# Cross-attention and an int8-style feed-forward: key products by seven block products for eight, sums and scaling on GpSimd, one pool of PSUM banks, a new order of steps

## The chip, the cores and the metric

The kernel runs on one core of a Trainium2 chip. The metric is the device time of one execution in microseconds (us), the median of several runs. The core has a matmul engine (TensorE, "PE" in the profile, its weight loads "PEld"), a vector engine (VectorE, "DVE"), an activation engine (ScalarE, "ACT"), a general engine (GpSimd, "POOL") and a queue that issues all DMAs here (SyncE, "SP"). Matmul results land in PSUM, which has eight banks of 512 fp32 columns per partition; everything else lies in SBUF or in DRAM.

## The reference, cut to what matters

Eight batches of 112 tokens of 512 features attend to a context of 375 rows of 256 features, and then go through a feed-forward layer with operands rounded as if to int8. There are 16 heads of 128.

```python
def attention(x, ctx):                  # x is layer-normed, per batch
    q = (x @ Wq).reshape(Sq, 16, 128)
    k = (ctx @ Wk).reshape(375, 16, 128)
    v = (ctx @ Wv).reshape(375, 16, 128)
    q, k = rmsnorm(q, gq), rmsnorm(k, gk)          # over each head's 128
    p = softmax(q k^T / sqrt(128))                 # per head
    return (p v).reshape(Sq, 2048) @ Wo
x = x + attention(layernorm(x), ctx)
x = x + ffn(layernorm(x))               # rows of x and all of W1, W2 scaled and rounded to +-127,
                                        # gelu between, hidden width 2048
```

## The kernel before

The batches go in four pairs p. The heads go in four groups of 4 heads (512 columns of Wq, Wk, Wv). A pair and a group of heads make one of 16 groups G; a group and one of its two batches make one of 32 units u. All of it is fp32 up to the feed-forward layer; each fp32 matmul of the program shows as two in the profile.

For one unit: `keys` multiplies three tiles of 128 context rows (the context is padded from 375 to 384) with the group's 512 columns of Wk, each tile in two products that accumulate over the 256 features (L650). `key_keep` copies the tile out of PSUM (ScalarE, L670), `key_squares` squares it (ScalarE, L675), `key_sums` adds the squares per head (VectorE, L681), the root steps (names `ka`, `kb`, `ke`, `kd`: Ln and Exp on ScalarE, small VectorE operations) make 1/rms, `key_norm` scales the tile (VectorE, L688), `key_blocks` transposes its blocks of 32 (VectorE, L698), `key_send` writes them to DRAM in four DMAs and `key_fetch` reads them back as the transposed keys kT. For the very first unit the transposition is done on TensorE. `queries` makes q in the same manner (L532); the 112 tokens of the last batch lie in the 16 spare rows of the other seven batches' tiles of 128, so it needs no query products of its own. `scores` multiplies q and kT (L758, one bank per head), `score_max` finds maxima in PSUM (VectorE, L771), `score_exp` takes the exponential (ScalarE, L780), `scale_probs` divides by the sum (ScalarE, L791), `prob_blocks`, `prob_send` and `prob_fetch` transpose the probabilities by way of DRAM (pz, pd, pT). `weigh` multiplies the probabilities with the context itself (L860), `weigh_keep` copies the result (L871); per group, `values` multiplies it with Wv (L887), `value_keep` copies, `project` multiplies with Wo (L910) and `project_add` sums the groups in aT (VectorE, L926). When a pair's four groups are done, the result is transposed back, added to x, normalized, rounded and sent through the feed-forward layer (`hidden` L1080, `gelu` L1096, `output` L1159). The last unit and the last two batches use TensorE transposes in place of those through DRAM.

Tiles are taken from pools with a fixed number of buffers; a new tile of a tag waits until the oldest one's readers are done. The context tiles cT and c have 3 buffers each, the key tiles 2 of three tiles. PSUM is divided into two pools of 4 banks: `ps_sc` for score tiles and `ps_mm` for all else. GpSimd does four memsets at the start and two maxima over partitions.

The order is written out by hand. `step` gives each piece of work a short name (k0..k2 `keys`, kc `key_keep`, kq `key_squares`, kr `key_sums`, kn `key_norm`, kt `key_blocks`, ks and kf the DMAs, s `scores`, x `score_max`, e `score_exp`, n `scale_probs`, w `weigh`, o `values`, p `project`, h `hidden`, g and ge `gelu`, f.. the feed-forward statistics). `play` runs through a script of such words, `name.number`, once for each pair, and `in_written_order` then ties every instruction of TensorE, VectorE, ScalarE and SP to the one before it on its engine. So each engine works strictly in the script's order, and an instruction that waits holds all behind it on its engine.

## Time and profile before

| | us |
|---|---|
| median of 3 runs | 721.83 |
| lowest, highest | 721.05, 722.44 |
| span of the profiled execution | 718.5 |
| TensorE busy | 702.7 |
| VectorE busy | 537.3 |
| ScalarE busy | 433.6 |
| GpSimd busy | 2.4 |
| key products (L650) | 171.8 |
| weighing (L860) | 152.3 |
| projection (L910) | 101.8 |
| queries (L532) | 100.2 |
| scores (L758) | 92.4 |

The span runs from the first to the last instruction of the one execution that was profiled; the profile has no time of that execution around the span. Busy time is a union of intervals, and the ends of matmuls are modelled, so a matmul that stands alone looks longer than one in a row. "Idle before" is time that an engine waited ahead of a group of instructions, with what ended the wait.

### The profile page before, as it was taken

The page shows a single profiled execution, that of the slowest core. Times are in us where ns is not written, and L with a number is a line of the kernel's source. Part 1 is how long each engine was busy: PE and PEld are TensorE (multiplying, and loading weights), DVE is VectorE, ACT ScalarE, POOL GpSimd, SP SyncE. Part 2 cuts the span into 40 slices and gives each one's busy share as a digit, 9 for nine tenths or more (in the row PEclk, how much of TensorE's full clock was granted, in tenths as well). Part 3 has the DMA queues.
Part 4 walks back from the last instruction along what each step waited for, and adds up shares of the span by engine and source line. Part 5 has one row for each costly group of instructions (what it writes and reads, how often), then busy time and mean ns, then how long its engine had stood idle before and what let it go on. Part 6 is the DMA issues. An engine that isn't in the chain of part 4 may idle for free.

```text
span 718.5 us, 8555 instructions
## 1 busy us (share of the span) xinstructions
PE 702.7 (98%) x2398; PEld 413.3 (58%) x2410; DVE 537.3 (75%) x1234; ACT 433.6 (60%) x1129; POOL 2.4 (0%) x10
## 2 busy tenths in 40 slices
PE   9999999999999999999999999999999999999976
PEld 4444456655657564745656465564657455667742
DVE  6997888887876677747857787868774898964395
ACT  5677576636475756556466556666755566627325
POOL 0000000000000000000000000000000000000000
PEclk9999999999999999999999999999999999999999
DMA  8799999989988999999898989999999889998201
GB/s 304 266 280 298 294 298 282 301 268 290 282 308 244 293 285 313 269 275 310 227 289 286 295 265 287 287 240 305 292 257 291 237 256 272 259 290 282 34 1 44
DMA packets 131246, 187.85 MB, mean 261 GB/s; under 512 B 34864, under 2 KB 90800, under 8 KB 130560
## 3 DMA queue, kind: packets, MB, share of 16 engines
q1 hardware_dynamic: 131200, 187.32, 85.1%
q8 instruction: 19, 0.31, 0.2%
q14 instruction: 27, 0.22, 0.1%
HBM read 124.55 MB, written 59.45 MB: 256 GB/s over the span
## 4 chain that ended last, share of the span: by engine, by line
PE 85%; DVE 5%; ACT 4%; DMA 3%; SPq 1%; issue 1%; POOL 0%; ACTq 0%; DVEq 0%; POOLq 0%
PE pkk L650 19%; PE pu L860 17%; PE pw L910 13%; PE pq L532 12%; PE sc L758 10%; PE po L887 6%; PE py L1159 2%; PE ph L1080 2%; DMA pT<-pd 1%; PE pkk L660 1%; DMA kT<-kd 1%; ACT probs L780 1%; DMA qr<-q 1%; DMA qss<-s 1%; ACT qsq L547 1%
## 5 line engine op out<-in xcount | busy, mean ns | idle before, releaser
L650 PE MATMUL pkk<-wk,cT 128*128 128x512 f32 x372 | 171.8, 593 | 0.3 <-DVE hid L1089 0.3
L860 PE MATMUL pu<-pT,c 128*128 128x448 f32 (+1 forms) x384 | 152.3, 540 | 1.0 <-DMA pT<-pd 1.0
L860 PEld LDWEIGHTS pu<-pT,c 128*128 128x128 f32 (+1 forms) x384 | 72.5, 190 | 71.3 <-issue 61.7
L780 ACT ACTIVATE probs<-sc,bias,rq 112x375 f32<-112x375 f32 x128 | 84.1, 663 | 47.8 <-DVE bias L773 47.8
L650 PEld LDWEIGHTS pkk<-wk,cT 128*128 128x128 f32 x372 | 70.0, 190 | 72.3 <-issue 60.9
L910 PEld LDWEIGHTS pw<-oT,wo 128*128 128x128 f32 x544 | 98.2, 190 | 9.8 <-issue 6.5
L910 PE MATMUL pw<-oT,wo 128*128 128x224 f32 (+1 forms) x544 | 101.8, 343 | 0.6 <-ACT oT L897 0.6
L532 PE MATMUL pq<-wq,xnT 128*128 128x512 f32 x224 | 100.2, 592 | 0.0
L758 PE MATMUL sc<-kT,qT 128*112 128x384 f32 x256 | 92.4, 486 | 0.3 <-DMA kT<-kd 0.2
L670 ACT COPY kk<-pkk 128x512 f32<-128x512 f32 x96 | 55.2, 580 | 58.6 <-DVE kz L698 25.6
L797 DVE STREAM_TRANSPOSE pz<-probs 128x384 f32<-128x384 f32 x120 | 63.7, 558 | 21.1 <-ACT probs L791 18.2
L791 ACT ACTIVATE probs<-probs,inv 112x375 f32<-112x375 f32 x128 | 72.1, 605 | 8.9 <-DVE inv L788 8.9
L771 DVE TENSOR_REDUCE top<-sc 112x1 f32<-112x375 f32 x128 | 63.8, 535 | 18.0 <-PE sc L758 17.5
L681 DVE TENSOR_REDUCE kss<-ksq 128x4 f32<-128x512 f32 x96 | 63.1, 668 | 14.0 <-ACT ksq L675 14.0
L532 PEld LDWEIGHTS pq<-wq,xnT 128*128 128x128 f32 x224 | 42.4, 190 | 49.6 <-issue 46.5
L758 PEld LDWEIGHTS sc<-kT,qT 128*112 128x112 f32 x256 | 44.7, 177 | 38.9 <-issue 16.7
L675 ACT ACTIVATE ksq<-kk 128x512 f32<-128x512 f32 x96 | 59.5, 628 | 6.4 <-DVE kss L681 6.0
L688 DVE TENSOR_TENSOR kk<-kk,rk 128x512 f32<-128x512 f32 x96 | 62.9, 675 | 0.5
L698 DVE STREAM_TRANSPOSE kz<-kk 128x512 f32<-128x512 f32 x93 | 62.3, 690 | 0.9 <-issue 0.4
L871 ACT COPY wc<-pu 128x448 f32<-128x448 f32 x64 | 33.5, 531 | 36.6 <-PE pu L860 36.6
L887 PEld LDWEIGHTS po<-wc,wv 128*128 128x128 f32 x272 | 49.1, 190 | 8.0 <-issue 4.1
L887 PE MATMUL po<-wc,wv 128*128 128x224 f32 (+1 forms) x272 | 53.1, 344 | 0.0
(122 smaller groups left out, 590.8 us busy)
## 6 DMA issues: line engine op xcount, KB each, us to landing
kd<-kz SPq DMA_DIRECT2D x124, 192.0 KB, 4.0
kT<-kd SPq DMA_DIRECT2D x31, 768.0 KB, 6.4
pT<-pd SPq DMA_DIRECT2D x30, 672.0 KB, 6.1
pd<-pz SPq DMA_DIRECT2D x90, 192.0 KB, 4.4
wq<-in_wq SPq DMA_DIRECT2D x16, 1024.0 KB, 7.7
wo<-in_wo SPq DMA_DIRECT2D x16, 1024.0 KB, 7.8
wv<-in_wv SPq DMA_DIRECT2D x16, 512.0 KB, 5.8
wk<-in_wk SPq DMA_DIRECT2D x15, 512.0 KB, 6.2
```

Of the source, the lines that this page charges most:

```text
L532: nc.tensor.matmul(pq[:, :GW], T["xnT", p][:, k, i * P : (i + 1) * P], T["wq", G][:, k, :], start=(k == 0), stop=(k == KC - 1),)
L650: nc.tensor.matmul(pk[:, :GW], T["cT", batch_of(u)][:, k, j * P : (j + 1) * P], T["wk", u // BP][:, k, :], start=(k == 0), stop=(k == KCC ...
L681: nc.vector.tensor_reduce(T["kss", u][:, j, :], T.pop(("ksq", u, j)).rearrange("p (h d) -> p h d", d=D), AX.X, ALU.add)
L688: nc.vector.tensor_tensor(kv, kv, T["rk", u][:, j, :].unsqueeze(2).to_broadcast([P, HG, D]), ALU.mult)
L758: nc.tensor.matmul(sc[:S, :SKP].rearrange("p (j i r) -> p j i r", j=NJ, r=BK), T["qT", G, i][:, h, :], T["kT", u][:, :, :, h, :].rearrange ...
L771: nc.vector.tensor_reduce(top[:, h : h + 1], T["sc", u, h0 + h][:S, :SK], AX.X, ALU.max, negate=True)
L780: nc.scalar.activation(p_bufs[h][:S, :SK], T["sc", u, h][:S, :SK], AF.Exp, bias=T["bias", u, h0][:, h - h0 : h - h0 + 1], scale=rq_of(u, h ...
L791: nc.scalar.mul(p_bufs[h][:S, :SK], p_bufs[h][:S, :SK], T["inv", u][:, h : h + 1])
L797: nc.vector.transpose(T["pz", u][:, :, :, :, h, :].rearrange("p a f j q -> p j a f q"), p_bufs[h].rearrange("p (j a r) -> p j a r", j=NJ, ...
L860: nc.tensor.matmul(pu[:, : HG * S], T["c", b][: ROWS[j], j, k * P : (k + 1) * P], T["pT", u][: ROWS[j], :, j, :, :].rearrange("p f h q -> ...
L887: nc.tensor.matmul(po[:, (h - h0) * n : (h - h0 + 1) * n], T["wv", G][:, k, h * D : (h + 1) * D], T["wc", G][:, k, h, :, :].rearrange("p b ...
L910: nc.tensor.matmul(pw[:, (c - c0) * n : (c - c0 + 1) * n], T["wo", G][:, h, c * P : (c + 1) * P], T["oT", G][:, h, lo : lo + n], start=(h ...
```

## The change

For all groups but the first, `keys` is replaced. A pair of batches has 2 x 3 tiles of context rows; they are taken as three pairs of tiles n = 0, 1, 2. For a pair of tiles the left factor is a 2 x 2 block matrix (two row tiles, two halves of the 256 features), and so is the right one (two halves of the features, two halves of the 512 columns). In place of eight block products of 128 x 128 by 128 x 256 there are seven, of blocks and of sums of blocks. `context_sums` and `weight_sums` make the sums on GpSimd, once per pair of batches and once per group; two of the sums overwrite blocks of cT and wk. Products 1, 6 and 7 accumulate in one bank kX, and ScalarE copies it after each of them (`chain_keep`); products 4, 5, 3 and 2 land in another bank kR, lower tile first (`low_products`), then, when the lower tile has been read, upper tile (`high_products`). VectorE adds the copies to kR and so makes the key tiles (`low_keep`, `high_keep`).

The scaling of the keys (`key_norm`) moves from VectorE to GpSimd for all units but the first two. GpSimd's instructions are now tied to the written order too. The two PSUM pools become one of 8 banks. cT and c get 2 buffers in place of 3, the key tiles 3 buffers of two tiles; a few small tiles share buffers. One script with all units in it replaces the four, with every step placed anew; the number of DMAs is the same. In it `context_sums` of the pairs 1 to 3 comes after `rows_blocks` (cb), which reads the same cT. Near the end ScalarE does the Ln and Exp of batch 7's statistics after the Gelus of batch 6.

```diff
--- before.py
+++ after.py
@@ -23,7 +23,7 @@
 
 
 ENG = mybir.EngineType
-ORDERED = (ENG.PE, ENG.DVE, ENG.Activation, ENG.SP)
+ORDERED = (ENG.PE, ENG.DVE, ENG.Activation, ENG.SP, ENG.Pool)
 LOG_EXP = "natural_log_exp_and_others"
 
 
@@ -90,8 +90,7 @@
     work = ctx.enter_context(tc.tile_pool(name="work", bufs=2))
     ffn = ctx.enter_context(tc.tile_pool(name="ffn", bufs=1))
     dram = ctx.enter_context(tc.tile_pool(name="dram", bufs=2, space=bass.MemoryType.DRAM))
-    ps_mm = ctx.enter_context(tc.tile_pool(name="ps_mm", bufs=4, space=PSUM))
-    ps_sc = ctx.enter_context(tc.tile_pool(name="ps_sc", bufs=4, space=PSUM))
+    ps_mm = ctx.enter_context(tc.tile_pool(name="ps_mm", bufs=8, space=PSUM))
 
     def mm_tile(name):
         return ps_mm.tile([P, NW], F32, tag="mm", name=name)
@@ -117,8 +116,8 @@
 
 
     ident = const.tile([P, P], F32, name="ident")
-    ramp = const.tile([P, BK], F32, name="ramp")
-    ramp_t = const.tile([P, BK], F32, name="ramp_t")
+    ramps = work.tile([P, 2 * BK], F32, tag="qsq", name="ramps", bufs=1)
+    ramp, ramp_t = ramps[:, :BK], ramps[:, BK:]
     nc.vector.memset(ramp[:, :1], 0.0)
     nc.vector.memset(ident, 0.0)
     n = 1
@@ -234,7 +233,7 @@
         T["wo", G] = t
 
     def pad_context(b):
-        t = work.tile([P, KCC, SKP], F32, tag="cT", name=f"cT_{b}", bufs=3)
+        t = work.tile([P, KCC, SKP], F32, tag="cT", name=f"cT_{b}", bufs=2)
         nc.vector.memset(t[:, :, SK:], 0.0)
         T["cT", b] = t
 
@@ -476,7 +475,7 @@
 
     def rows_keep(b, j0, j1):
         if j0 == 0:
-            T["c", b] = work.tile([P, NJ, CC], F32, tag="c", name=f"c_{b}", bufs=3)
+            T["c", b] = work.tile([P, NJ, CC], F32, tag="c", name=f"c_{b}", bufs=2)
         nc.scalar.copy(
             T["c", b][:, j0:j1, :].rearrange("p j c -> p (j c)"), T.pop(("pc", b))[:, : (j1 - j0) * CC]
         )
@@ -508,7 +507,7 @@
 
     def rows_order(b, k):
         if k == 0:
-            T["c", b] = work.tile([P, NJ, CC], F32, tag="c", name=f"c_{b}", bufs=3)
+            T["c", b] = work.tile([P, NJ, CC], F32, tag="c", name=f"c_{b}", bufs=2)
         nc.scalar.copy(
             T["c", b][:, :, k * P : (k + 1) * P].rearrange("p j (b c) -> p j b c", c=BK),
             T["cr", b][:, :, :, k, :].rearrange("p b j c -> p j b c"),
@@ -662,17 +661,130 @@
                 start=(k == 0), stop=(k == KCC - 1),
             )
 
+    def keys_at(u, j):
+        G, i = divmod(u, BP)
+        n, m = (1, i) if j == NJ - 1 else (BP * i, j)
+        return keys_of(G, n)[:, m, :]
+
+    def keys_of(G, n):
+        if ("kk", G, n) not in T:
+            T["kk", G, n] = work.tile([P, 2, GW], F32, tag="kk", name=f"kk_{G}_{n}", bufs=3)
+        return T["kk", G, n]
+
     def key_keep(u, j):
         if u == 0:
             after(("kh", 1))
-        if ("kk", u) not in T:
-            T["kk", u] = work.tile([P, NJ, GW], F32, tag="kk", name=f"kk_{u}")
-        nc.scalar.copy(T["kk", u][:, j, :], T["pkk", u, j][:, :GW])
+        nc.scalar.copy(keys_at(u, j), T["pkk", u, j][:, :GW])
+
+    HW = GW // 2
+
+    def tile_pair(G, n):
+        b = G // NG * BP
+        return (((b, 0), (b, 1)), ((b, 2), (b + 1, 2)), ((b + 1, 0), (b + 1, 1)))[n]
+
+    def block_of(G, n, r, k):
+        b, j = tile_pair(G, n)[r]
+        return T["cT", b][:, k, j * P : (j + 1) * P]
+
+    def context_sums(p, n):
+        G = p * NG
+        b, j = tile_pair(G, n)[1]
+        after(("cb0" if p > 0 else f"ct{j // 2}", b))
+        a11, a12, a21, a22 = [block_of(G, n, r, k) for r in range(2) for k in range(KCC)]
+        t = T["cs3", p, n] = work.tile([P, 3, P], F32, tag="cs3", name=f"cs3_{p}_{n}", bufs=3)
+        s1, s2, s4, s3 = t[:, 0, :], t[:, 1, :], t[:, 2, :], a21
+        nc.gpsimd.tensor_tensor(s1, a21, a22, ALU.add)
+        nc.gpsimd.tensor_tensor(s3, a11, a21, ALU.subtract)
+        nc.gpsimd.tensor_tensor(s2, s1, a11, ALU.subtract)
+        nc.gpsimd.tensor_tensor(s4, a12, s2, ALU.subtract)
+
+    def weight_sums(G):
+        w = T["wk", G]
+        b11, b12, b21, b22 = [w[:, k, h * HW : (h + 1) * HW] for k in range(KCC) for h in range(2)]
+        t = T["wt3", G] = wpool.tile([P, 3, HW], F32, tag="wt3", name=f"wt3_{G}")
+        t1, t2, t4, t3 = t[:, 0, :], t[:, 1, :], t[:, 2, :], b12
+        nc.gpsimd.tensor_tensor(t1, b12, b11, ALU.subtract)
+        nc.gpsimd.tensor_tensor(t3, b22, b12, ALU.subtract)
+        nc.gpsimd.tensor_tensor(t2, b22, t1, ALU.subtract)
+        nc.gpsimd.tensor_tensor(t4, b21, t2, ALU.subtract)
+
+    def factors(G, n, m):
+        if m > 2:
+            after(("tT", G), (f"tS{n}", G // NG))
+        a11, a12, s3, a22 = [block_of(G, n, r, k) for r in range(2) for k in range(KCC)]
+        b11, t3, b21, b22 = [T["wk", G][:, k, h * HW : (h + 1) * HW] for k in range(KCC) for h in range(2)]
+        if m < 3:
+            return ((a11, b11), (a12, b21))[m - 1]
+        t, c = T["wt3", G], T["cs3", G // NG, n]
+        return (
+            (c[:, 2, :], b22), (a22, t[:, 2, :]), (c[:, 0, :], t[:, 0, :]), (c[:, 1, :], t[:, 1, :]), (s3, t3)
+        )[m - 3]
+
+    def product(G, n, m, to, start, stop):
+        lhs, rhs = factors(G, n, m)
+        nc.tensor.matmul(to, lhs, rhs, start=start, stop=stop, skip_group_check=True)
+
+    def chain_product(G, n, m):
+        if m == 1:
+            T["kX", G, n] = mm_tile(f"kX_{G}_{n}")
+        product(G, n, m, T["kX", G, n][:, :HW], m == 1, m == 7)
+
+    def chain_keep(G, n, m):
+        if m != 7 and ("ke", G, n) not in T:
+            T["ke", G, n] = work.tile([P, 2, HW], F32, tag="ksq", name=f"ke_{G}_{n}")
+        if m == 7:
+            T["kf", G, n] = work.tile([P, 1, HW], F32, tag="ksq", name=f"kf_{G}_{n}")
+            to = T["kf", G, n][:, 0, :]
+        else:
+            to = T["ke", G, n][:, 0 if m == 1 else 1, :]
+        nc.scalar.copy(to, T["kX", G, n][:, :HW])
+
+    def low_products(G, n):
+        r = T["kR", G, n] = mm_tile(f"kR_{G}_{n}")
+        product(G, n, 4, r[:, :HW], True, True)
+        product(G, n, 5, r[:, HW:], True, False)
+
+    def high_products(G, n):
+        r = T["kR", G, n]
+        after((f"cL{n}", G))
+        product(G, n, 3, r[:, HW:], False, True)
+        product(G, n, 2, r[:, :HW], True, True)
+
+    def low_keep(G, n):
+        after((f"mL{n}", G), (f"n7{n}", G))
+        nc.vector.tensor_tensor(
+            keys_of(G, n)[:, 1, :].rearrange("p (a c) -> p a c", a=2), T["kR", G, n].rearrange("p (a c) -> p a c", a=2),
+            T["kf", G, n].to_broadcast([P, 2, HW]), ALU.add,
+        )
+
+    def high_keep(G, n):
+        after((f"mH{n}", G), (f"n6{n}", G), (f"n1{n}", G))
+        nc.vector.tensor_tensor(
+            keys_of(G, n)[:, 0, :], T["kR", G, n], T["ke", G, n].rearrange("p a c -> p (a c)"), ALU.add
+        )
+
+    step("tT", NG, weight_sums)
+    for n in range(NJ):
+        step(f"tS{n}", 1, context_sums, n)
+        step(f"mL{n}", NG, low_products, n)
+        step(f"mH{n}", NG, high_products, n)
+        step(f"cL{n}", NG, low_keep, n)
+        step(f"cH{n}", NG, high_keep, n)
+        for m in (1, 6, 7):
+            step(f"m{m}{n}", NG, chain_product, n, m)
+            step(f"n{m}{n}", NG, chain_keep, n, m)
+
+    def kept(u, j):
+        G, i = divmod(u, BP)
+        if G == 0:
+            return f"kc{j}", u
+        n, m = (1, i) if j == NJ - 1 else (BP * i, j)
+        return f"c{'HL'[m]}{n}", G
 
     def key_squares(u, j):
-        after((f"kc{j}", u))
+        after(kept(u, j))
         sq = T["ksq", u, j] = work.tile([P, GW], F32, tag="ksq", name=f"ksq_{u}_{j}")
-        nc.scalar.activation(sq, T["kk", u][:, j, :], AF.Square)
+        nc.scalar.activation(sq, keys_at(u, j), AF.Square)
 
     def key_sums(u, j):
         if ("kss", u) not in T:
@@ -683,9 +795,9 @@
         )
 
     def key_norm(u, j):
-        after(("kd", u), (f"kc{j}", u))
-        kv = T["kk", u][:, j, :].rearrange("p (h d) -> p h d", d=D)
-        nc.vector.tensor_tensor(
+        after(("kd", u), kept(u, j))
+        kv = keys_at(u, j).rearrange("p (h d) -> p h d", d=D)
+        (nc.vector if u < BP else nc.gpsimd).tensor_tensor(
             kv, kv, T["rk", u][:, j, :].unsqueeze(2).to_broadcast([P, HG, D]), ALU.mult
         )
 
@@ -697,12 +809,12 @@
             )
         nc.vector.transpose(
             T["kz", u][:, :, j, :, :].rearrange("p a h r -> p h a r"),
-            T["kk", u][:, j, :].rearrange("p (h a r) -> p h a r", h=HG, r=BK),
+            keys_at(u, j).rearrange("p (h a r) -> p h a r", h=HG, r=BK),
         )
 
     def key_send(u):
         after(*[(f"kt{j}", u) for j in range(NJ)])
-        kd = T["kd", u] = dram.tile([NB, BK, NB, NJ * HG * BK], F32, tag="kd", name=f"kd_{u}")
+        kd = T["kd", u] = dram.tile([NB, BK, NB, NJ * HG * BK], F32, tag="kd", name=f"kd_{u}", bufs=3)
         for i in range(NB):
             nc.sync.dma_start(
                 out=kd[:, :, i, :].rearrange("a d n -> d a n"),
@@ -722,7 +834,7 @@
         after((f"kn{j}", u))
         pt = T["pkt", u, j] = mm_tile(f"pkt_{u}_{j}")
         for h in range(HG):
-            nc.tensor.transpose(pt[:, h * P : (h + 1) * P], T["kk", u][:, j, h * D : (h + 1) * D], ident)
+            nc.tensor.transpose(pt[:, h * P : (h + 1) * P], keys_at(u, j)[:, h * D : (h + 1) * D], ident)
 
     def key_place(u, j, copy):
         if ("kT", u) not in T:
@@ -754,7 +866,7 @@
     def scores(u, h):
         G, i = divmod(u, BP)
         after((f"G{i}" if G > 0 else f"qx{i}", G))
-        sc = T["sc", u, h] = ps_sc.tile([P, NW], F32, tag="sc", name=f"sc_{u}_{h}")
+        sc = T["sc", u, h] = ps_mm.tile([P, NW], F32, tag="mm", name=f"sc_{u}_{h}")
         nc.tensor.matmul(
             sc[:S, :SKP].rearrange("p (j i r) -> p j i r", j=NJ, r=BK), T["qT", G, i][:, h, :],
             T["kT", u][:, :, :, h, :].rearrange("p i j r -> p j i r"), start=True, stop=True,
@@ -939,10 +1051,10 @@
     NF4 = F // NW
     HALF = KF // 2
     HOMES = dict(
-        xq=(ffn, "xq", 1), xqT=(ffn, "xqT", 1), hid=(ffn, "hid", 1), hq=(ffn, "hq", 1), hqT=(ffn, "hqT", 1)
+        xq=(ffn, "hq", 1), xqT=(ffn, "xqT", 1), hid=(ffn, "hid", 1), hq=(ffn, "hq", 1), hqT=(ffn, "hqT", 1)
     )
     LAST_HOMES = dict(
-        xq=(work, "ksq", 2), xqT=(work, "ksq", 2), hid=(wpool, "wo", 1), hq=(work, "kk", 2), hqT=(work, "kz", 1)
+        xq=(work, "ksq", 2), xqT=(work, "ksq", 2), hid=(wpool, "wo", 1), hq=(work, "kk", 3), hqT=(work, "kz", 1)
     )
 
     def home(what, b, shape, dtype):
@@ -971,7 +1083,7 @@
     def sum_blocks(b):
 
         p, i = divmod(b, BP)
-        after(("az", p), ("a0", p * NG + NG - 1), ("a1", p * NG + NG - 1))
+        after(*([("az", p)] if i else []), ("a0", p * NG + NG - 1), ("a1", p * NG + NG - 1))
         t = T["rz", b] = work.tile([P, NB, KC, BK], F32, tag="qz", name=f"rz_{b}", bufs=1)
         nc.vector.transpose(
             t.rearrange("p i k c -> p k i c"),
@@ play: four scripts of steps become one @@
-    play("""
...
-    """, 0)
...
+    play("""
...
+    """)
     in_written_order()
```

## The prediction

> **What bounds the kernel now.** First the page: the span, the busy time of each engine, the chain that ended last by engine and by line.
>
> ```profile
> span 718.5 us, 8555 instructions
> PE 702.7 (98%) x2398; PEld 413.3 (58%) x2410; DVE 537.3 (75%) x1234; ACT 433.6 (60%) x1129; POOL 2.4 (0%) x10
> ...
> PEclk9999999999999999999999999999999999999999
> ...
> q1 hardware_dynamic: 131200, 187.32, 85.1%
> ...
> PE 85%; DVE 5%; ACT 4%; DMA 3%; SPq 1%; issue 1%; POOL 0%; ACTq 0%; DVEq 0%; POOLq 0%
> PE pkk L650 19%; PE pu L860 17%; PE pw L910 13%; PE pq L532 12%; PE sc L758 10%; PE po L887 6%; PE py L1159 2%; PE ph L1080 2%; DMA pT<-pd 1%; PE pkk L660 1%; DMA kT<-kd 1%; ACT probs L780 1%; DMA qr<-q 1%; DMA qss<-s 1%; ACT qsq L547 1%
> ```
>
> TensorE is the bound, and the key products (L650), which the change touches, are its largest share. A busy PE is not yet a PE at its rate, so next the chain in order of time (start, length, work), from which I take prices, and the waits of TensorE:
>
> ```profile
> 179.08 6.05 PE pw L910 x32
> 204.24 4.52 PE pu L860 x12
> 235.78 3.45 PE pq L532 x8
> 246.31 3.43 PE pkk L650 x8
> ```
> ```profile
> PE pxq L1052 <- DVE xq L1039: 3.2, 1, 3.2
> PE phq L1052 <- ACT hq L1137: 1.6, 3, 0.8
> PE warm L116 <- POOL probs L111: 1.2, 1, 1.2
> PE pu L860 <- DMA pT<-pd: 1.0, 1, 1.0
> ```
>
> Each fp32 product is two matmuls. One matmul of 224 columns costs 6.05/32 = 189 ns, of 448 columns 4.52/12 = 377, of 512 columns 3.43/8 = 429: price is proportional to columns. The waits are small, and two of the four largest lie at the end. Hence the stretches (columns: length, PE, PEld, DVE, ACT, POOL busy with counts, clock, DMA share):
>
> ```profile
> 360.00:460.00 100.00, 99.89 (x319) 57.01 (x320) 73.10 (x173) 65.08 (x181) 0.00 (x0) 1.00 0.89 282
> 460.00:560.00 100.00, 99.32 (x349) 61.43 (x351) 69.56 (x156) 58.65 (x141) 0.00 (x0) 1.00 0.97 281
> 560.00:660.00 100.00, 98.75 (x342) 59.76 (x345) 78.79 (x183) 61.27 (x148) 0.00 (x0) 1.00 0.88 260
> 660.00:718.00 58.00, 47.08 (x276) 30.44 (x277) 37.23 (x82) 23.79 (x46) 0.00 (x0) 0.99 0.21 53
> ```
>
> Up to 660 us TensorE is full; the last 58 us are a chain over all engines with 11 us of TensorE idle. A saved matmul is worth its price before 660 and much less after. So the change has two questions: how much work leaves TensorE where it is full, and whether the new order keeps it full.
>
> **The change, part by part.** *Products.* 180 of the 186 products of L650 go (360 matmuls of 512 columns): 360 x 0.429 = -154.4 us. 15 groups x 3 pairs of tiles x 7 products x 2 = 630 matmuls of 256 columns come, at 189 + 32 x (377-189)/224 = 216 ns: +136.1. Net -18.3. A weight load takes 190 ns, so it still fits under 216.
>
> *Where it leaves.* I added these prices along TensorE's order of both kernels, up to the last score product of the last unit (a unit is one group of heads of one batch) and behind it: 647.6 and 45.8 us before, 639.7 and 35.2 after. So the new order also draws other work forward: the full part shrinks by 7.9, the end by 10.6. The end is a chain. Before, the last score leaves TensorE at 657.4, the weighing of its unit starts at 670.98, the last addition to aT at 686.17, the end is 718.5. After, the order puts 7.8 us of TensorE work between score and weighing where 13.6 passed; by rows the chain there is two maxima 1.1, bias 0.2, two exponentials 1.7, inverse 0.2, four scalings 2.4, transposes and copies 1.5, handoffs 1: 8.1 to 10. Weighing 4.5, its copy 0.5, values 2.0, copy 0.5, three hidden products 2.6, projection 3.0 and handoffs give about 23.5 from score to aT, against 28.8: -5.3. But ScalarE now does batch 7's Ln and Exp after batch 6's four Gelus, and the order holds three more table loads there; two lie on batch 7's chain:
>
> ```profile
> L1096 ACT ACT_TABLE_LOAD x6 | 7.7, 1283 | 0.1
> ```
>
> 2 x 1.28 = 2.6, of which DVE, in its order, hides about 1.4 (before, 689.83 to 691.26 passed between Exp and its use). The end: -5.3 + 1.2 = -4.1.
>
> *VectorE and ScalarE.* Rows of the groups (busy, mean ns; idle before left to the reader):
>
> ```profile
> L688 DVE TENSOR_TENSOR kk<-kk,rk 128x512 f32<-128x512 f32 x96 | 62.9, 675 | 0.5
> L926 DVE TENSOR_TENSOR aT<-aT,pw 128x448 f32<-128x448 f32 x24 | 14.4, 610 | 13.2 <-PE pw L910 13.1
> L670 ACT COPY kk<-pkk 128x512 f32<-128x512 f32 x96 | 55.2, 580 | 58.6 <-DVE kz L698 25.6 <-PE pkk L650 25.4 <-PE sc L758 5.7
> L871 ACT COPY wc<-pu 128x448 f32<-128x448 f32 x64 | 33.5, 531 | 36.6 <-PE pu L860 36.6
> L111 POOL MEMSET probs<- 128x384 f32 x4 | 1.5, 418 | 0.3 <-POOLq L1390 0.3
> ```
>
> VectorE loses 90 scalings x 0.675 = -60.8 and gets 90 additions with one operand in PSUM, 0.68 each (610 at 448 columns): +61. ScalarE loses 90 x 0.58 = -52 and gets 135 copies of 256 columns, 0.38 by the slope between 448 and 512: +52. Both unchanged, neither the bound. SP issues the same DMAs (707 instructions on its queue either way), in another order; at 85.1% of a span 1% shorter the engines still have room.
>
> *GpSimd.* 90 scalings of 512 columns, 60 sums of 256, 48 of 128. No row shows one. Lower bound: VectorE's 0.675. Upper: memset writes 384 columns in 418 ns, a single column in 98, so 0.83 ns a column; two reads and a write one after another would be 0.1 + 3 x 0.43 = 1.38. I take 1.2, nearer to GpSimd's own row: 108 + 38 + 18 = 164 us, 23% of the span. The Trainium skill's GPSIMD Engine Reference, section 3.1, gives about 2.6 cycles per element for two inputs at 1.2 GHz, which would be an estimated 1.1 us.
> The scaling lies between the key's root and its block transpose, so each unit's chain to kT grows by 3 x (1.2-0.675) = 1.6 us; what queues behind is VectorE, whose transposes (L698) now wait in order for GpSimd, and behind them the score maxima.
>
> *New waits (from nothing to the far end).* I counted, at the prices above, the TensorE work that the new order leaves between producer and consumer.
> (a) One accumulating bank is copied out between products: product, copy, product. Before, po's last product ended 681.68, its copy ran 681.72 to 682.25, the next projection started 682.31: with 0.38 for the copy and the 0.16 a lone matmul shows beyond its rate, 0.65 must pass. 15 of the 45 second round trips get 0.58 to 0.86. ScalarE is 60% busy with operations of 0.6, so about 0.1 each: 1.5 (0 to 15 x 0.87 = 13).
> (b) Last score to weighing: before 14 to 55 us (median 34.5), after 8 to 42 (25.4). The chain by rows is 17.7; units 15, 17 and 30 get 17.3 to 17.7. Before, the products often stood within 2 us of the landing and TensorE waited 1.0 in all. I take 1 (0 to 15, were the chain the 21.5 of the shortest seen before).
> (c) Last key product to scores: median 53 before, 36 after. The chain is 20.2; units 24 to 26, where one pair of context buffers must be given back first, get 21.1, 21.8, 18.8: 1 (0 to 8).
> (d) One pool of 8 banks: 23 of 440 banks are taken again within 2 us of their last product, 12 before, mostly in the first 60 us: 0.5 (0 to 6).
> (e) GpSimd's program is exchanged four times more (around the two maxima over partitions): no row shows its length; 0.5 (0 to 8).
>
> A rule against the change: the trace has GpSimd idle, so it shows no meeting of the two engines. The Trainium skill's SBUF — State Buffer, "Who interferes with whom", says that a VectorE operation with two SBUF inputs and a GpSimd operation that reads SBUF block each other for the whole instruction. By it some 253 small operations (63 roots x 3, 64 biases) would each meet a busy GpSimd with chance 0.23 and lose 0.6: an estimated 35 us of VectorE, and the sum would be some 3 us higher.
>
> Sum: -7.9 - 4.1 + 1.5 + 1 + 1 + 0.5 + 0.5 = -7.5. Against the profiled span 718.5 that is 711.0; the page has no time around the span, and the median of the runs is 3.3 above it: 714.3; I write 714.
>
> **The rivals.** *Everything hidden.* The new waits are nothing and the end follows TensorE: the full -18.3, 703.5. For it: before, TensorE waited 3 us in 600. Against: the end was no TensorE chain before.
> *Short gaps.* (b) at its far end, (a) to (e) else a bit above my values: some +15 in place of 4.5, about 725. For it: every median gap shrank. Against: before's landings met their products closely.
> *GpSimd holds VectorE (slower).* Place: the key scaling ahead of L698. VectorE has 25 us in 100 to spare, 5.4 per unit of 21.9. If a scaling takes 1.2 + x, each chain grows by 3x. At x = 1 units 24 to 26 and 30 fall short by 2, 1.4, 4.4 and 0: +8, and the gain is gone, which is the point from which it decides; at x = 1.5 the shortages are 14 and VectorE's waits of 4.5 per unit begin to show at the maxima, some +20 in all: about 734. For it: no row bounds GpSimd against a busy VectorE. Against: even three passes give 1.38.
>
> **How the numbers follow.** My forecast (707 to 719) 0.42, everything hidden 0.17, short gaps 0.18, GpSimd 0.20, something else 0.03. Runs of before differ by 1.4 us, 0.2%, which is what can be told from no change. Faster: 0.41 + 0.17 + 0.04 + 0.02 = 0.64; same 0.05; slower 0.31. The range reaches from all hidden, 703, into the GpSimd case, 730; the forecast alone has 707 to 719.
>
> **What would show it.** Right: 630 matmuls of 256 columns at 0.21 to 0.22 us apart, TensorE busy near 684 with under 5 us more waits before the last score, GpSimd rows near 1.2 us, an end about 57 us long behind the last score. Wrong: rows of POOL among the releasers of VectorE's transposes with more than 1 us each; L650's successors waiting for ScalarE copies; pu or sc waiting for DMA near units 15, 17, 24 to 26, 30.

## The result: 9.7% slower

The changed kernel takes 790.34 us (median; 788.86 to 796.78) beside 721.44 us of the kernel before on the same chip: ratio 1.097, 95% interval 1.093 to 1.102. The range of the forecast ended at 730. The profiled execution has a span of 787.8 us, before 718.5. The ratios here leave out runs that are over 1.5% above the fastest of the same kernel (two of four in `a_noex`, one each in `a_eight` and `a_tmax_moved`); the medians keep them.

The page of the changed kernel (span, busy time, share of the queue, chain that ended last):

```profile
span 787.8 us, 9506 instructions
PE 713.8 (91%) x2680; PEld 467.3 (59%) x2680; DVE 569.4 (72%) x1234; ACT 440.9 (56%) x1177; POOL 161.6 (21%) x208
...
q1 hardware_dynamic: 131200, 187.32, 78.2%
...
PE 30%; DMA 29%; DVE 19%; ACT 9%; SPq 8%; issue 4%; POOL 1%; DVEq 0%; ACTq 0%; POOLq 0%
```

No engine is the bound any more. TensorE's share of the chain fell from 85% to 30%; transfers, VectorE and ScalarE alternate with it. TensorE stands idle for 74 us of the span (before 16). The waits of TensorE (us in total, times, longest):

```profile
PE pu L972 <- DMA pT<-pd: 12.1, 9, 2.5
PE pp L939 <- ACT probs L903: 9.9, 1, 9.9
PE kX L725 <- ACT ke L740: 8.7, 9, 1.9
PE kR L725 <- DVE kk L755: 6.7, 9, 2.4
PE pw L1022 <- ACT oT L1009: 5.9, 2, 5.2
```

There is one large wait, and otherwise many of 1 to 2 us behind a DMA, ScalarE and VectorE in turn. The stretches show that they lie everywhere (columns as in the prediction: length, busy of PE, PEld, DVE, ACT, POOL, clock, DMA share):

```profile
60.00:110.00 50.00, 39.64 (x122) 23.29 (x123) 42.72 (x94) 32.64 (x94) 14.43 (x16) 0.86 0.67 191
...
360.00:460.00 100.00, 94.98 (x348) 61.95 (x348) 67.64 (x143) 57.82 (x162) 18.27 (x20) 1.00 0.81 252
460.00:560.00 100.00, 92.99 (x331) 58.08 (x330) 76.16 (x163) 57.60 (x143) 14.31 (x18) 0.97 0.89 250
560.00:660.00 100.00, 93.62 (x369) 66.98 (x368) 71.44 (x163) 58.38 (x162) 26.83 (x34) 0.98 0.83 248
```

Before, TensorE was busy for at least 98.75 us in each of the three long ones; now for 93 to 95, and the granted clock is below full in three of the four. Split at the last score product by the timeline: it ends at 733.5 us (before 657.4), and what follows takes 54.3 us (before 61.0). So 76 us were lost ahead of it and 7 gained behind it.

### The profile page after: what moved, and what is told of

It reads as the page before. It is cut to its first block, busy times and chain, and to the rows that moved or that the text cites. A ratio compares the mean times of both kernels' runs of the same rounds, so it can differ in the third digit from the quotient of the medians.

```text
span 787.8 us, 9506 instructions
## 1 busy us (share of the span) xinstructions
PE 713.8 (91%) x2680; PEld 467.3 (59%) x2680; DVE 569.4 (72%) x1234; ACT 440.9 (56%) x1177; POOL 161.6 (21%) x208
## 4 chain that ended last, share of the span: by engine, by line
PE 30%; DMA 29%; DVE 19%; ACT 9%; SPq 8%; issue 4%; POOL 1%; DVEq 0%; ACTq 0%; POOLq 0%
DMA pT<-pd 6%; PE pu L972 6%; PE pw L1022 6%; PE sc L870 4%; DMA kd<-kz 4%; DMA pd<-pz 3%; PE kR L725 3%; PE pq L531 3%; DMA qd<-qz 3%; DMA rd<-rz 3%; DVE kz L810 2%; PE ph L1192 2%; PE kX L725 2%; DVE pz L909 2%; SPq L819 2%
## 5 line engine op out<-in xcount | busy, mean ns | idle before, releaser
L972 PE MATMUL pu<-pT,c 128*128 128x448 f32 (+1 forms) x384 | 159.9, 557 | 18.1 <-DMA pT<-pd 12.1
L800 POOL TENSOR_TENSOR kk<-kk,rk 128x512 f32<-128x512 f32 x90 | 93.0, 1059 | 283.2 <-DVE rk L370 196.4
L1022 PE MATMUL pw<-oT,wo 128*128 128x224 f32 (+1 forms) x544 | 105.6, 349 | 5.9 <-ACT oT L1009 5.9
L1022 PEld LDWEIGHTS pw<-oT,wo 128*128 128x128 f32 x544 | 99.9, 194 | 11.2 <-ACT oT L1009 6.9
L531 PE MATMUL pq<-wq,xnT 128*128 128x512 f32 x224 | 101.8, 597 | 0.0
L870 PE MATMUL sc<-kT,qT 128*112 128x384 f32 x256 | 98.1, 495 | 2.9 <-ACT probs L892 1.1
L810 DVE STREAM_TRANSPOSE kz<-kk 128x512 f32<-128x512 f32 x93 | 62.6, 689 | 16.2 <-POOL kk L800 13.6
L725 PE MATMUL kX<-wk,cT 128*128 128x256 f32 x180 | 54.1, 391 | 6.4 <-ACT ke L740 5.3
L999 PE MATMUL po<-wc,wv 128*128 128x224 f32 (+1 forms) x272 | 54.9, 347 | 2.1 <-ACT probs L892 1.0
L740 ACT COPY ke<-kX 128x256 f32<-128x256 f32 x90 | 33.1, 368 | 38.0 <-PE kX L725 25.5
L725 PEld LDWEIGHTS kX<-wk,cT 128*128 128x128 f32 x180 | 33.5, 193 | 25.2 <-ACT ke L740 9.6
```

Of the source, the lines that this page charges most:

```text
L531: nc.tensor.matmul(pq[:, :GW], T["xnT", p][:, k, i * P : (i + 1) * P], T["wq", G][:, k, :], start=(k == 0), stop=(k == KC - 1),)
L725: nc.tensor.matmul(to, lhs, rhs, start=start, stop=stop, skip_group_check=True)
L800: (nc.vector if u < BP else nc.gpsimd).tensor_tensor(kv, kv, T["rk", u][:, j, :].unsqueeze(2).to_broadcast([P, HG, D]), ALU.mult)
L810: nc.vector.transpose(T["kz", u][:, :, j, :, :].rearrange("p a h r -> p h a r"), keys_at(u, j).rearrange("p (h a r) -> p h a r", h=HG, r=BK),)
L870: nc.tensor.matmul(sc[:S, :SKP].rearrange("p (j i r) -> p j i r", j=NJ, r=BK), T["qT", G, i][:, h, :], T["kT", u][:, :, :, h, :].rearrange ...
L972: nc.tensor.matmul(pu[:, : HG * S], T["c", b][: ROWS[j], j, k * P : (k + 1) * P], T["pT", u][: ROWS[j], :, j, :, :].rearrange("p f h q -> ...
```

## The experiments

Times are medians with the ratio to the kernel before on the same chip. Three theories stood against each other: single parts of the change cost it (GpSimd, the seven products, the bank pool), the halved clock does, or the order does.

**Single parts taken back out of the changed kernel.** `a_kn_dve`: the scaling of the keys goes back to VectorE.

```diff
-        (nc.vector if u < BP else nc.gpsimd).tensor_tensor(
+        nc.vector.tensor_tensor(
```

> The changed kernel with the key scaling of all groups on VectorE (90 instructions of 0.675 us back, 61 us), the 26 sums still on GpSimd, order untouched. STOP: VectorE no longer waits for GpSimd directly, so 15 to 30 us go, 760 to 775, although VectorE's queue is 61 us longer. PORT: VectorE gets back its 32 us and the kernel with it, 755 or less. ORDER: 785 to 800, the longer VectorE queue on the same short distances.

Measured 791.62 us, 1.095 [1.091, 1.100]: the time of the changed kernel, but with two things changed. The largest wait of TensorE in the list above (9.9 us) and one of 5.2 us are gone here, because VectorE no longer stands behind GpSimd there; that alone is worth 15 us (`a_tmax` below). VectorE is busy for 604.3 us, 35 more, and in this order that costs about as much. Set against `a_tmax`, the scaling on VectorE costs some 16 us.

`a_all_dve`: the block sums go to VectorE too (each `nc.gpsimd.tensor_tensor` of `context_sums` and `weight_sums` becomes `nc.vector.tensor_tensor`).

> The changed kernel with the key scaling and the sums on VectorE: GpSimd does what it did in the kernel before (the all-reduce alone). What is left of the 68 us is then the order, the seven products and the one pool of banks. STOP: within 10 us of the run with the scaling alone on VectorE. PORT: under 745. ORDER: 780 or more.

798.15 us, 1.107 [1.102, 1.111]: 8 us worse, again without the two waits, and with VectorE busy for 628.3 us. With no elementwise work on GpSimd at all a loss of this size is still there, so GpSimd holding VectorE is not the main cause. It is the cause of those two waits.

`a_eight`: the changed kernel's order with eight products again. Two products of 512 columns per tile stand where `mL` and `mH` stood, VectorE copies the result where it added, and the steps of products 1, 6 and 7, their copies and the sums are empty.

```diff
-        product(G, n, 4, r[:, :HW], True, True)
-        product(G, n, 5, r[:, HW:], True, False)
+        eight(G, n, 1)
...
-            step(f"m{m}{n}", NG, chain_product, n, m)
-            step(f"n{m}{n}", NG, chain_keep, n, m)
+            step(f"m{m}{n}", NG, lambda G, n, m: None, n, m)
+            step(f"n{m}{n}", NG, lambda G, n, m: None, n, m)
```

> The changed kernel with the keys of all groups by eight products again: the words of products 4 and 5 and of products 2 and 3 issue two products of 512 columns for one tile each, the words of products 1, 6 and 7, of their copies and of the sums issue nothing, the words of the two adds are plain copies on VectorE; the key scaling stays on GpSimd. TensorE has 18 us more to do, ScalarE 52 us less, and no product waits for a copy. If the round trips of the seven products cost more than they save (ORDER): 790 or less. If the loss is elsewhere (STOP, PORT): 795 to 808.

788.25 us (780.35 to 792.94), 1.089 [1.082, 1.096]. TensorE is busy for 730.0 us, 16 more than in the changed kernel, and the time is the same within the intervals. But the two waits are gone here too: without the block sums GpSimd takes its first maximum at 43.9 us in place of 53.9. The fair partner is `a_tmax`, with seven products and without these waits: 1.072. So in this order the seven products are worth some 12 us, with their sums, copies and round trips, where 18 were forecast.

`a_eight_dve`: `a_eight` with all the scaling on VectorE. Of the change only the order, the one pool of banks and the buffers remain (two for three of each context tile, three of two key tiles each for two of three, small tiles that share); TensorE has the products of the kernel before, GpSimd nothing new. Two things are of this run alone: the copies of the keys take 61 us on VectorE in place of 52 on ScalarE, so that VectorE is 56 us busier than before, and two key tiles still follow each other in one bank kR.

> The changed kernel with eight products (as in the run of that name) and with all key scaling on VectorE: every engine has the work that it had before, GpSimd the all-reduce alone. What is left of the change is the written order, the one pool of banks and the two buffers for a context instead of three. Theory ORDER (the new order by itself makes waits, whatever is computed): 770 to 790, with 60 us of idle TensorE. Theory PARTS (products and GpSimd make the waits): 735 or less, as TensorE's work is that of before. A replay of the engines' queues in the order of the program, with the mean durations of the profile's rows, gives 778 here and 725 for the kernel before.

794.6 us, 1.100 [1.095, 1.104]. Its page and its two largest waits of TensorE:

```profile
span 794.2 us, 8579 instructions
PE 729.9 (92%) x2395; PEld 416.9 (52%) x2410; DVE 593.2 (75%) x1324; ACT 400.6 (50%) x1042; POOL 2.4 (0%) x10
```
```profile
PE pu L971 <- DMA pT<-pd: 19.7, 9, 3.6
PE kR L744 <- DVE kk L759: 14.0, 13, 2.9
```

A loss of the whole size is there without the seven products, without GpSimd's new work and without the two waits. Part of it may be the run's own: the 14.0 us are products that wait for VectorE's copies out of kR, which the kernel before does not have.

**The same parts in the old order.** `b_kn_pool`: the kernel before with the scaling on GpSimd and GpSimd tied to the order.

```diff
-ORDERED = (ENG.PE, ENG.DVE, ENG.Activation, ENG.SP)
+ORDERED = (ENG.PE, ENG.DVE, ENG.Activation, ENG.SP, ENG.Pool)
...
-        nc.vector.tensor_tensor(
+        (nc.vector if u < BP else nc.gpsimd).tensor_tensor(
```

> The kernel before, in its own order, with the key scaling of all groups but the first on GpSimd: 90 instructions of 1.06 us there for 0.675 us on VectorE, and GpSimd changes between all-reduce and tensor_tensor. Theory STOP: two stops of 5 to 10 us, 730 to 745 (the replay gives 741). If the stop needs the new order: within 5 us of before. If VectorE's lightening pays: under 718.

722.51 us, 1.0006 [0.9994, 1.0017]:

```profile
span 721.4 us, 8604 instructions
PE 704.2 (98%) x2398; PEld 413.2 (57%) x2410; DVE 496.1 (69%) x1144; ACT 434.3 (60%) x1129; POOL 97.6 (14%) x100
```

VectorE is 41 us less busy and GpSimd 95 us more, and nothing moves: TensorE remains full at 98%.

`b_pool`: the kernel before with one pool of eight banks (`ps_mm` with `bufs=8`, `scores` takes its tile from it).

> The kernel before with one pool of eight PSUM banks for two pools of four, nothing else. ORDER and PARTS both: within 3 us of before (the replay gives 1 us less), so that the pool is off the list. If banks handed over round a ring of eight are what stands TensorE: 730 or more.

721.97 us, 0.999 [0.998, 1.001]. The pool costs nothing in the old order. Two context buffers could not be tried there, since the old order would then wait for itself; so order and buffers are not told apart from each other.

**The one large wait.** The 9.9 us wait in the list stands at 66.7 us. The timeline there, of GpSimd and of those behind it (start, length, instruction, idle before it with the releaser):

```profile
53.88 0.38 POOL L321 PARTITION_ALL_REDUCE absw<-pm_w  x1 [6.30 <-DVE bias L885]
61.48 3.03 POOL L800 TENSOR_TENSOR kk<-kk,rk 128x512 f32<-128x512 f32 x3 [7.22 <-issue]
63.54 0.71 DVE L810 STREAM_TRANSPOSE kz<-kk 128x512 f32<-128x512 f32 x1 [10.62 <-POOL kk L800]
64.86 0.63 ACT L787 ACTIVATE ksq<-kk 128x512 f32<-128x512 f32 x1 [10.42 <-DVE kss L793]
66.69 0.82 PE L939 MATMUL pp<-ident,probs 112*128 112x112 f32 x3 [9.88 <-ACT probs L903]
```

Around each maximum over partitions the trace has instructions named MODIFY_POOL_CONFIG (ten in all, before two); I read them as the exchange of GpSimd's program between the maximum and the elementwise operations. After the maximum GpSimd waits 7.22 us for nothing that the profile shows; VectorE's transpose (L810) waits for the scaling with its queue behind it, then ScalarE, then TensorE. `a_noex` takes the maximum out of GpSimd; the maximum over partitions, which scales the rounded weights, is left out.

```diff
-        nc.gpsimd.partition_all_reduce(absmax, pm1, P, bass.bass_isa.ReduceOp.max)
+        nc.vector.tensor_copy(absmax, pm1)
```

> The changed kernel, but the maximum over the partitions of each weight is left out (VectorE copies the column of maxima; each row is then scaled by its own), so that GpSimd never changes between the all-reduce and tensor_tensor. Theory STOP (each change of GpSimd's program stands the in-order VectorE, and with it the kernel, for about 10 us at 53 us and 8 us at 165 us, and TensorE's granted clock is 0.91 to 0.96 in the stretches behind them): the time falls by 20 to 35 us, to 755 to 770 us, and the count of how far TensorE lags behind its work no longer jumps at 54 and 165 us. Theory ORDER (the new order puts dependent steps too close, product to copy to product above all): at most 5 us less, 785 to 790. Theory PORT (VectorE's small operations stretched by GpSimd's tensor_tensor, +32 us of busy VectorE): 785 to 790 too, as the 90 scalings stay on GpSimd.

775.85 us, 1.066 [1.056, 1.076]: 14.5 us gone by the medians, some 22 by the ratios; the four runs spread from 763.68 to 778.64.

`a_tmax` computes the maximum in another way: a TensorE transpose of the column, a VectorE maximum over the row, and a product that spreads it.

> The changed kernel with the maximum over the partitions taken by a TensorE transpose, a VectorE maximum and a product that spreads it, in place of GpSimd's all-reduce, twice, at the same words of the order; all else as in the changed kernel. STOP as far as the run without the maximum went (15 us less than the changed kernel): 770 to 780. If the short round trip TensorE, VectorE, TensorE at these two words costs as much as the exchange: 785 to 792.

775.25 us, 1.072 [1.069, 1.076]: 15 us gone, and this is the better measure of the exchange. It is the fastest kernel found with the new order and nothing left out, and still 7% behind the kernel before.

**The halved clock.** In the changed kernel the granted clock drops to 0.50 for 3 us or more after nine gaps of TensorE. Summing busy time x (1 - clock) over stretches of 1 us gives 17.1 us of lost rate (before 0.0). `a_fill` puts 191 idle products of 128 columns ahead of the nine instructions that wait there, so that TensorE stays busy.

```diff
+    def fill(n):
+        pt = mm_tile(f"fill_{n}")
+        for _ in range([8, 72, 11, 12, 36, 11, 12, 13, 16][n]):
+            nc.tensor.matmul(pt[:, :P], ident, ident, start=True, stop=True)
```

> The changed kernel with idle products put into TensorE's queue ahead of nine instructions that the trace of the changed kernel shows waiting 1.9 to 9.9 us, 8 to 72 fp32 products of 128 columns (0.11 us each) at a place, each time about 1 us less than the gap; nothing reads what they compute. Theory CLOCK (the trace shows the granted clock at 0.50 for 3 to 10 us after each of the nine gaps of 1.9 us and more, 17 us of TensorE's work lost to it in all): the gaps are filled, the clock stays at 1.00, and 8 to 17 us go, 773 to 782. If what TensorE does after a gap has time anyhow, since it waits again soon: 786 to 792. If the filler itself delays the work behind it: over 792.

The clock is full throughout, and the time is 791.48 us, 1.096 [1.092, 1.101]: nothing. My reading is that a TensorE that works off its rows faster only arrives earlier at the next wait; the run does not exclude that the idle products took back part of what the clock gave. As it stands, the low clock does not explain the loss.

**What is short in the new order.** Transfers are 29% of the chain. `a_three` is the changed kernel without the exchange on GpSimd (as `a_noex`), without the key scaling from the second group on, and with the fetches of kT and pT reading the send of the unit before, so that they wait for no fresh data.

```diff
-            in_=T.pop(("pd", u)).rearrange("a r f n -> (a r) (f n)"),
+            in_=T["pd", u - 1 if ("pd", u - 1) in T else u].rearrange("a r f n -> (a r) (f n)"),
```

> The changed kernel with three suspects out at once: the maximum over the partitions left out (no change of GpSimd's program), the key scaling left out for all groups but the first (no GpSimd on the path, no 90 instructions), and the fetches of turned keys and probabilities reading what the unit before sent (no wait for the last send). Theory ORDER (no single resource is late; the written order leaves TensorE's inputs no margin on any of ScalarE, VectorE and the transfers): still 750 to 770, with 50 us of idle TensorE. If GpSimd with its exchange and the waits for the transfers were the cause together: 730 or less.

763.24 us, 1.058 [1.054, 1.062], 12 us under `a_tmax`; pu still waits 13.3 us for pT. Shorter chains help a little.

`a_light` loads only a quarter of Wq and Wo from the third group on (the products take that quarter four times, so queries and projections have other values but the same work): 165 MB for 187.

```diff
-        nc.sync.dma_start(out=t, in_=wq[:, bass.ts(G % NG, GW)].rearrange("(k p) n -> p k n", p=P))
+        k = KC if G < 2 else 1
+        nc.sync.dma_start(out=t[:, :k, :], in_=wq[: k * P, bass.ts(G % NG, GW)].rearrange("(k p) n -> p k n", p=P))
...
-                pq[:, :GW], T["xnT", p][:, k, i * P : (i + 1) * P], T["wq", G][:, k, :],
+                pq[:, :GW], T["xnT", p][:, k, i * P : (i + 1) * P], T["wq", G][:, k if G < 2 else 0, :],
```

> The kernel after, with a quarter of Wq and of Wo loaded for all groups but the first two (256 KB in place of 1024 KB each; the products take that one quarter in place of all four, so queries and projection are left out in their values but not in their work). 42 of 187 MB of transfers go; the instructions of all engines stay. Theory (the new order runs without margin against its transfers, which come late whenever the 16 DMA engines are busy): faster by some 20 us of 790, ratio to the kernel before about 1.07 (1.05 to 1.08), and the waits of pu for pT become smaller than the 12 us they had. Rival (the gaps come from chains through VectorE, ScalarE and GpSimd in strict order, and the transfers are only where they show): within 5 us of the kernel after, ratio 1.09 to 1.10.

771.5 us, 1.066 [1.062, 1.071]: 19 us gone (the expectation's 42 MB to go were 22 by the page). pu's wait for pT stayed at 12.1 us, so the wait's name did not tell what the transfers cost.

The DMA queue itself waits more too. All DMAs are issued in order, and the loads of weights now stand for products that still read the tile to be overwritten: 47 us in 28 waits, before 6 us in 4. The largest of them, in the changed kernel and then in the kernel before (us in total, times, longest):

```profile
SPq L217 <- PE kR L725: 17.7, 8, 4.7
SPq L211 <- PE pq L531: 16.7, 5, 6.8
```
```profile
SPq L212 <- PE pq L532: 4.2, 2, 4.0
```

In `a_eight_dve` it is 50 us in 27, so this comes with the order and its buffers. What it costs in time was not measured.

`b_light`, the same in the kernel before:

> The kernel before with the same quarter loads. Both theories: TensorE is the bound and what it waits for is not transfers, so no change, 718 to 723 us, ratio 0.995 to 1.002. A gain of more than 5 us would say that the old order also waits for transfers, and the comparison with the changed kernel would tell nothing.

718.8 us, 0.9955 [0.994, 0.997]. Here it is worth 3.5 us.

`a_heavy` and `b_heavy` go the other way: one more transfer of 256 KB per group, 2% of the traffic, into the tile of Wq that the transfer just ahead of it fills.

```diff
+        nc.sync.dma_start(out=t[:, :1, :], in_=wq[:P, bass.ts(G % NG, GW)].rearrange("(k p) n -> p k n", p=P))
```

> The kernel after with one more transfer of 256 KB per group: the first quarter of Wq is loaded a second time (16 transfers, 4 of 187 MB, 2% more; the values stay). Theory (no margin): the cost is several times that of the same addition in the kernel before; by the replay of the queues +67 us, which is a rough figure, so +25 to +70: ratio 1.13 to 1.19. Rival (transfers are not what is short): +0 to +10 us, ratio 1.095 to 1.11, no more than in the kernel before.

> The kernel before with the same second load of a quarter of Wq per group. Theory (the old order holds margin against its transfers): the addition costs 0 to 17 us, ratio 1.00 to 1.024, a third or less of what it costs in the changed kernel. Rival (the two orders have the same margin, and the changed one loses its time elsewhere): both kernels lose the same number of us within 5.

`a_heavy` 849.62 us, 1.177 [1.172, 1.181], +59; `b_heavy` 761.79 us, 1.055 [1.051, 1.059], +39. Neither expectation held for the kernel before: it loses two thirds of what the changed one does. But the edit does more than add traffic. The second load waits until the first has landed, with every other DMA behind it; these are the waits of the queue in `b_heavy` and in `a_heavy`:

```profile
SPq L213 <- DMA wq<-in_wq: 116.0, 16, 9.7
```
```profile
SPq L212 <- DMA wq<-in_wq: 98.2, 16, 8.5
```

So the two runs measure sixteen stops of the DMA queue, 6 to 7 us in the mean, and not 2% of traffic alone. Under them the page of the kernel before moves toward that of the changed one:

```profile
PE 718.0 (95%) x2410; PEld 416.3 (55%) x2410; DVE 538.0 (71%) x1234; ACT 435.3 (57%) x1129; POOL 2.4 (0%) x10
...
PE 45%; DMA 21%; DVE 16%; ACT 8%; SPq 8%; issue 3%; DVEq 0%; ACTq 0%
```

Both orders lose when fetches come late, the new one more. How close the old order stands to a loss from traffic alone is not shown. `a_tmax_light` and `a_three_light` ask whether the gains add: `a_tmax` and `a_three` with the quarter loads.

> The kernel after with the maximum over partitions by a TensorE transpose (no exchange of GpSimd's program) and the quarter loads of Wq and Wo together. Theory A (two separate losses): the gains add, 14 us of the exchange and 19 of the transfers, 790 - 33 = 757 (752 to 761), ratio 1.043 to 1.055, and some 35 us over the kernel before stay for chains over engines. Theory B (one and the same shortage seen twice): well short of the sum, 763 to 771, ratio 1.057 to 1.07.

> The kernel after without the exchange, without the scaling of the keys on GpSimd, with the fetches of kT and pT reading the send of the unit before (their values are wrong, their place in the queues is kept), and with the quarter loads. What still stands between a send and the products is then only VectorE's and ScalarE's own work in its strict order and the transfer itself. Theory A: the gains add, 763 - 19 = 744 (739 to 750), ratio 1.024 to 1.04. Theory B (what is left are chains of VectorE and ScalarE, which neither transfers nor GpSimd touch): 752 to 763, ratio 1.042 to 1.057.

755.36 us, 1.048 [1.044, 1.052], and 744.37 us, 1.031 [1.026, 1.037]. The gains of the exchange and of the light loads add, to 2 us. What TensorE still waits for in `a_three_light`:

```profile
PE pu L977 <- DMA pT<-pd: 7.7, 6, 2.8
PE kX L728 <- ACT ke L743: 7.1, 8, 2.4
PE phq L1169 <- ACT hq L1254: 3.4, 3, 3.0
```

**Another order.** I replayed the queues from the programs' order and the mean durations of the rows: each engine in its order, the program's waits, one pipe for transfers. It gives 725 us for the kernel before (span 718.5), 778 for `a_eight_dve` (794.2), 764 for `a_tmax` (777.4) and 741 for `b_kn_pool` (721.4), so it is right to some 3%. A search over it moved 541 of 2783 words of `a_tmax`'s script, to 742 from 764 in the replay (`a_tmax_moved`), and 64 of 2482 words of the old script, to 718 from 726 (`b_moved`).

> The same instructions, buffers and engines as in the run with TensorE's maximum; only the written order differs: 541 of its 2783 words stand elsewhere, each moved past words that it does not depend on, so that in the replay of the queues with the mean durations of the rows TensorE's idle time falls from 59 to 48 us and the end from 764 to 742. ORDER: the chip follows, 15 to 25 us less than the unmoved one, 750 to 760. If the loss is in the work and the buffers and not in the order: within 5 us of the unmoved one.

> The kernel before with 64 of its 2482 words moved in the same way; nothing else differs. The replay gives 718 in place of 726. ORDER, where the bound is TensorE's work and 15 us of idle time, most of it at both ends: 3 to 8 us faster, 714 to 719. If the replay is no guide for single microseconds: 720 to 725.

791.58 us, 1.094 [1.091, 1.098], and 722.04 us, 1.001 [0.999, 1.003]. The order tuned on mean durations is 16 us worse than the one it came from, where the replay gave 22 us of gain. So the order alone, with work and buffers the same, moves the time by 16 us, and a replay that is right to 3% cannot choose it.

## Why the prediction was wrong

**The step that failed** is the one under "New waits": counting the TensorE work that the new order leaves between producer and consumer, and setting it against a chain added up from rows (17.7 us from last score to weighing, 20.2 for the keys). Its terms came to 4.5 us; ahead of the last score 76 us were lost where the working had 3 to 4 gained (-7.9 and the waits). On the chip the chain is longer than its rows. By the timeline of the changed kernel, from a unit's last maximum to the issue of its pT fetch alone 16.6 us pass (median of 30 units; 10.8 to 26.1, a quarter above 21.8), and the fetch lands 5.9 us later: 22.5 where 17.7 was set for more than that. The order leaves 25.4 (median; 8 to 42), so the unit in the middle has little margin and many have none. The length of the chain alone does not tell the two kernels apart: before, the same stretch takes 21.9 and 6.1 us (medians), longer still, against a median of 34.5 that the order left. What differs is what remains at its end: a unit's weighing starts within 0.15 us of the landing of its fetch in 14 of 30 units, before in 2. That each instruction of the chain stands in an engine's queue behind others that wait, and that waits so feed each other, is how I explain it; no run takes it apart. I took units one by one; the shortage is common to all. "Every median gap shrank", which I wrote for the rival of short gaps, was the right reading; its price, +15, was a fifth of what it cost. Two more terms failed. The transfers were put at nothing ("the engines still have room"), and 22 of 187 MB less gain 19 us, where the kernel before gains 3.5. The exchange on GpSimd was put at 0.5 us, and costs 15.

**Where the 69 us come from,** by the runs: the exchange of GpSimd's program takes 15 (`a_tmax`). The order with its buffers takes the rest, 54 us (721.7 to 775.25), and more than that, since `a_tmax` has in it what the seven products save. `a_eight_dve`, which does without them, has +72, with VectorE's 56 us more in it. Read from the other end, 15 us go with the exchange, 19 with an eighth of the traffic, 11 to 12 with the scaling and the wait for fresh data together, which leaves 23 over the kernel before in `a_three_light`. What makes up these 23 is open: chains through VectorE and ScalarE, or the buffers. The old order with the seven products was not tried either.

**Point by point.**
- Price of the products: right. Two matmuls of 256 columns take 0.43 us in TensorE's timeline (361.90 to 362.33), 216 ns each; TensorE is 16 us less busy than in `a_eight` (18.3 forecast). Worth: some 12 us in the new order (`a_eight` against `a_tmax`). TensorE is busy for 713.8 us where 684 were set; 17 of the 30 are the halved clock.
- The end: -4.1 forecast, -6.8 measured.
- VectorE and ScalarE: the additions take 0.68 and the copies 0.37 us, as forecast. But VectorE is 32 us busier, see below.
- GpSimd: 1.06 us for a scaling (1.2 taken, within 0.675 to 1.38), 161.6 us busy in all (164 forecast). The total is close in part by luck: the scalings took 93 for 108, the sums 68 for 56.
- (a) round trips of the one bank: 1.5 taken, 8.7 in the list of waits. (b) 1 taken, 12.1 in the list. (c) 1 taken, and TensorE stood 2.9 us ahead of score products in all. (d) the pool: right, nothing in the old order.
- (e) exchange: 0.5 taken, 0 to 8 bounded; 15 in the new order, 0 in the old one, where the scaling ran on GpSimd around the same maximum (`b_kn_pool`). I had bounded the exchange but not asked what stood behind it in VectorE's order at 54 us. One sign that I had set for being wrong showed just this: VectorE's transposes waited 13.6 us for GpSimd, 10.6 of them here.
- The rule on VectorE and GpSimd, by the Trainium skill's SBUF — State Buffer, "Who interferes with whom": seen. VectorE's rows for the query roots went from 167 to 474 ns (L371 before, L370 after) and back to 166 in `a_all_dve`. Its estimate of 35 us of VectorE is near the 32, in part by luck: the last step of the key roots, counted among the 253, kept its 171 ns, and operations with one tensor operand, not counted, lengthened too (TENSOR_SCALAR of 112x8, 211 to 367 ns). Its estimate of 3 us on the end is not shown: no run takes the meetings away without putting work on VectorE.

These are the rows of the groups for the scaling and for that root in the changed kernel, and of the root before (busy, mean ns | idle before):

```profile
L800 POOL TENSOR_TENSOR kk<-kk,rk 128x512 f32<-128x512 f32 x90 | 93.0, 1059 | 283.2 <-DVE rk L370 196.4 <-DVE rs_u L368 30.9 <-DVE inv L900 17.0
L370 DVE SCALAR_TENSOR_TENSOR rq<-rs_u,rs_g 112x8 f32<-112x8 f32 x16 | 7.6, 474 | 0.5
```
```profile
L371 DVE SCALAR_TENSOR_TENSOR rq<-rs_u,rs_g 112x8 f32<-112x8 f32 x16 | 2.7, 167 | 0.5
```

## What to carry to other kernels

Where every engine works in a written order, a new order is a change of its own, and the largest: run the old work in the new order, and the new work in the old order, before counting what the new work saves. Compare how close behind the landing of their data the products start, in the timeline of each order, and do not set margins against chains that are added up from rows; when every margin shrinks, price the loss over all units and not only those that fall short. When a run takes one part out, look whether its largest waits are those of the kernel it is compared with: here four such runs also lost two waits that are worth 15 us, and two that were to add traffic stopped the DMA queue. And an order tuned to mean durations may have spent just the slack that the chip's variations need; that last is a guess from one run.

## What the hardware showed that was not expected

- GpSimd stood for 7.22 and 5.86 us around its two maxima over partitions before or after it took up elementwise work. The Trainium skill's GPSIMD Engine Reference, section 2.1, has about 6 us for the first call of freshly loaded code; 5.86 agrees, and 7.22 is longer.
- The granted clock fell to 0.50 after TensorE gaps of 1.88, 2.23, 2.36, 2.48 and 2.49 us, among others, and some of 1.4 to 1.96 us left it full. The Trainium skill's TensorE: Matmul & The Clock Gate, "What's actually happening", puts an idle window of about 3.4 us ahead of the lower clock; here shorter gaps were enough.
- A second load into a tile whose first load had not landed held the DMA queue of the kernel before 16 times, 116 us in all, and with its 4 MB cost it 39 us.
